# A selective-scan layer with experts: the sum over states moved from GpSimd adds to accumulating DMAs

## The chip, the cores and the metric

The kernel runs on one core of a Trainium2 chip. The metric is the device time of one execution in microseconds (us). The engines are named as in the profile: PE is TensorE (matrix products; PEld is its weight load), DVE is VectorE, ACT is ScalarE, POOL is GpSimd, SP is the engine that issues most DMAs.

## What is computed

The input x has 16 samples of 256 positions with 256 features, all float32. Each sample is normalised to xn, and the output is x plus a selective-scan branch plus a mixture of experts:

```python
proj = jnp.einsum('blh,he->bel', xn, W_in)
hidden, gate = jnp.split(proj, 2, axis=1)               # 512 features each
hidden = silu(causal_conv4(hidden, conv_kernel) + conv_bias)
ssm_p = jnp.einsum('ble,ed->bld', hidden.transpose(0, 2, 1), W_x)
dt, Bm, Cm = jnp.split(ssm_p, [128, 128 + 16], axis=-1)
dts = softplus(jnp.einsum('blr,re->ble', dt, W_dt) + b_dt)
dA  = exp(dts[..., None] * A)                           # A = -exp(A_log), 16 states
dBu = dts[..., None] * Bm[:, :, None, :] * hidden_ble[..., None]
# over positions: state = dA * state + dBu;  y = sum over the 16 states of state * Cm
y = (y + hidden * D) * silu(gate)
branch = jnp.einsum('bel,eh->blh', y, W_out)
# experts: 32 of them, 96 wide, the 8 most probable per position, weights renormalised;
# each adds ((silu(xn @ w_gate) * (xn @ w_up)) @ w_down) * weight
out = x + branch + experts
```

## The kernel before, in words

Samples are worked on one after the other, with the preparation of a sample laid under the scans of the one before. The 512 features of the scan are four chunks of 128 partitions, and the 256 positions lie along the free dimension. All experts are computed for all positions, as 24 chunks of 128 hidden features in 12 pairs (q), issued in 6 batches of two pairs.

The scan of a sample is cut into 16 units. A unit is one chunk c and one group g of NG = 4 states; a unit has two halves (h) of two states. One half is one slot of the plan, so a sample has 32 slots. For each unit:

- `fetch` has SP broadcast the rows of B (tile br) and of C (tile cr) of a group from a DRAM copy (bcd) to all partitions, 512 KB each.
- `feed` (L487) on POOL multiplies br by the chunk of hs, which `inputs` (L467) has turned from hidden to dts * hidden; the result is bu.
- `decay` (L502) on ACT writes exp(dts * A) of two states into a PSUM tile da. There are three of these (AHEAD = 3).
- `scan` (L511) on DVE runs the recurrence over a half in place in da, 512 elements a partition. The first position of each state has its decay forced to zero, which parts the two states.
- `read` (L522) on DVE multiplies da by cr into a half of the SBUF tile pr.
- `collect` (L536, L537, L538) on POOL adds the four states of pr to each other and to y: first 512 elements, then 256, then 256 into y. The tile y begins as hidden * D, written by `skip` (L462) on ACT.

After a sample's scans, `gate` (L546) makes the gate projection on PE into a PSUM bank, `gate_silu` (L555) applies SiLU in place on ACT, `gated` (L559) multiplies it into y on DVE, `project_out` (L565) adds the product with W_out on PE into the accumulator acc, and `finish` (L572) adds the x tile xt and stores the result. The accumulator also takes the experts' output (`down`, L374). The experts' products are made by `expand` (L343: pg and pu), `silu` (L351), `combine` (L356) and `weigh` (L362), which multiplies by the routing weights wr; `spread` (L329) broadcasts these from DRAM in six DMAs per quarter of the experts.

Before the scans of a sample: `stats`, `root`, `invert`, `norm`, `turn` (transposes, pt) and `keep_turned` (xnT) normalise it; `route`, `largest`, `expo`, `choose` route it; `project` (L385, ph), `conv_first` (L397, ACT) and `conv_rest` (L406, DVE) make the convolution into cv; `activate` (L413) writes hs; `params` (L422, px), `keep_params`, `widen` (L442, pdt) and `steps` (L454, dts by softplus) make the parameters.

The PSUM has three da tiles, two banks of kind g, two of kind u (`bank`), and acc. Products on PE share the g and u banks in turn, so a bank is free only when its reader is done: pgate of a sample is of kind u, like pu.

Each engine executes its own instructions in order. This order is written by hand: a dictionary WHEN gives each step a slot, relative to the first slot of its sample, and a rank inside the slot; the class Plan sorts by these and calls the steps. Nothing is reordered afterwards; the waits between engines follow from the tiles that the instructions read and write and from the number of buffers of the pools p1 to p4.

Of the kernel before, what the change touches and what calls it, by code (L numbers as in the profile page):

```python
# [34 lines left out]
def mamba_moe_kernel(  # L35
# [42 lines left out]
    NG = 4  # L78
    NH = 2
    HALVES = NG // NH  # L80
    AHEAD = 3
    GROUPS = N // NG
    UNITS = GROUPS * EC
    EPG = NE // GROUPS
    CPG = FC // GROUPS
    PAIRS = FC // 2
    BATCH = PAIRS // 6
    SLOTS = UNITS * HALVES
    SPG = EC * HALVES
    BATCH_AT = (8, 13, 19, 23, 29, 34)  # L90
# [4 lines left out]
        load_x=(-54, 34), stats=(-50, 35), root=(-49, 20), invert=(-48, 40), norm=(-47, 4),  # L95
        turn=(-46, 14), keep_turned=(-46, 14), route=(-39, 29), largest=(-38, 31), expo=(-37, 25),
        choose=(-37, 40), project=((-27, 32), (-24, 12)), conv_first=((-26, 4), (-24, 34)),
        conv_rest=((-24, 36), (-24, 20), (-22, 3), (-23, 35)), activate=(-22, 4), params=(-20, 10),
        keep_params=(-18, 9), turn_weights=(-19, 9), keep_weights=(-18, 11),
        widen=((-15, 9), (-13, 10)), steps=((-14, 34), (-13, 29)),  # L100
        skip=((-15, 8), (-9, 36), (-9, 16), (-9, 3)), inputs=(-7, 25), fetch=((-11, 8), (-6, 8)),
        spread=(6, 29), feed=(-2, 12), collect=(3, 34), gates=(1, 13), ups=(2, 9), silu=(2, 4),
        combine=((4, 8), (3, 34)), weigh=((5, 33), (4, 13)), down=(3, 14),
        gate=((27, 29), (33, 29)), gate_silu=((28, 14), (34, 6)), gated=((30, 31), (35, 34)),
        project_out=((37, 29), (39, 4)), finish=(47, 6),
# [20 lines left out]
    def load_x(b):  # L126
        xt = p4.tile([P, SPS, H], F32, tag="xt", name=f"xt_{b}")
        nc.sync.dma_start(xt, xf[ts(b, L), :].rearrange("(s p) h -> p s h", p=P))
        live["xt", b] = xt
# [34 lines left out]
    load_x(1)  # L164
# [226 lines left out]
    def conv_first(b, q):  # L391
        if q == 0:
            live["cv", b] = p1.tile([P, EC, L], F32, tag="cv", name=f"cv_{b}")
        cv, ph = live["cv", b], live["ph", b, q]
        for j in range(2):
            c = 2 * q + j
            nc.scalar.activation(  # L397
                cv[:, c, :], ph[:, j, :], AF.Identity,
                bias=cb[:, c, :], scale=cw[:, c, KC - 1 : KC],
            )  # L400

    def conv_rest(b, q, j):
        cv, ph = live["cv", b], live["ph", b, q]
        c = 2 * q + j
        for k in range(1, KC):
            nc.vector.scalar_tensor_tensor(  # L406
                cv[:, c, k:], ph[:, j, : L - k], cw[:, c, KC - 1 - k : KC - k],
                cv[:, c, k:], op0=ALU.mult, op1=ALU.add,
            )

    def activate(b):
        hs = p2.tile([P, EC, L], F32, tag="hs", name=f"hs_{b}")
        nc.scalar.activation(hs, live.pop(("cv", b)), AF.Silu)  # L413
        live["hs", b] = hs
# [43 lines left out]
    def skip(b, c):  # L458
        hs = live["hs", b]
        if c == 0:  # L460
            live["y", b] = p2.tile([P, EC, L], F32, tag="y", name=f"y_{b}")
        nc.scalar.activation(live["y", b][:, c, :], hs[:, c, :], AF.Copy, scale=dsk[:, c, :])  # L462
# [9 lines left out]
    def fetch(b, g, i):  # L472
        rep = p2.tile([P, NG, L], F32, tag="bc"[i] + "r", name=f"{'bc'[i]}r_{b}_{g}")
        rows = live["bcd", b][i * N + g * NG : i * N + (g + 1) * NG, :]
        nc.sync.dma_start(
            rep.rearrange("p n l -> p (n l)"),
            rows.rearrange("n l -> (n l)").partition_broadcast(P),
        )
        live["rep", b, g, i] = rep

    def unit(k):
        return k // UNITS, k // EC % GROUPS, k % EC

    def feed(k):
        b, g, c = unit(k)
        bu = p3.tile([P, NG, L], F32, tag="bu", name=f"bu_{b}_{g}_{c}")
        nc.gpsimd.tensor_mul(  # L487
            bu, live["rep", b, g, 0],
            live["hs", b][:, c : c + 1, :].to_broadcast([P, NG, L]),
        )  # L490
        live["bu", k] = bu

    def decay(m):
        k, h = divmod(m, HALVES)
        if k >= B * UNITS:
            return
        b, g, c = unit(k)
        dts = live["dts", b]
        da = ps_d.tile([P, NH, L], F32, tag="da", name=f"da_{b}_{g}_{c}_{h}")
        for j in range(NH):  # L500
            n = g * NG + h * NH + j
            nc.scalar.activation(  # L502
                da[:, j, :], dts[:, c, :], AF.Exp, scale=a_sb[:, c, n : n + 1]
            )
        live["da", m] = da

    def scan(m):
        k, h = divmod(m, HALVES)
        da = live["da", m]
        flat = da.rearrange("p n l -> p (n l)")  # L510
        nc.vector.tensor_tensor_scan(  # L511
            flat, flat, live["bu", k][:, ts(h, NH), :].rearrange("p n l -> p (n l)"), 0.0,
            op0=ALU.mult, op1=ALU.add,
        )

    def read(m):
        k, h = divmod(m, HALVES)
        b, g, c = unit(k)
        if h == 0:
            live["pr", k] = p3.tile([P, NG, L], F32, tag="pr", name=f"pr_{b}_{g}_{c}")  # L520
        cr = live["rep", b, g, 1]
        nc.vector.tensor_mul(  # L522
            live["pr", k][:, ts(h, NH), :], live.pop(("da", m)), cr[:, ts(h, NH), :]
        )
# [7 lines left out]

    def collect(k):
        b, g, c = unit(k)
        pr, y = live.pop(("pr", k)), live["y", b]
        nc.gpsimd.tensor_add(pr[:, 0:2, :], pr[:, 0:2, :], pr[:, 2:4, :])  # L536
        nc.gpsimd.tensor_add(pr[:, 0, :], pr[:, 0, :], pr[:, 1, :])  # L537
        nc.gpsimd.tensor_add(y[:, c, :], y[:, c, :], pr[:, 0, :])  # L538
# [14 lines left out]
    def gate_silu(b, q):  # L553
        pg = live["pgate", b, q]
        nc.scalar.activation(pg, pg, AF.Silu)  # L555

    def gated(b, q):
        y = live["y", b]
        nc.vector.tensor_mul(y[:, ts(q, 2), :], live.pop(("pgate", b, q)), y[:, ts(q, 2), :])  # L559

    def project_out(b, q):
        y, acc = live["y", b], live["acc", b]
        for c in range(2 * q, 2 * q + 2):
            for s in range(SPS):
                nc.tensor.matmul(  # L565
                    acc[:, s, :], y[:, c, ts(s, P)], wout_sb[:, c, :],
                    start=False, stop=False, skip_group_check=True,
                )

    def finish(b):  # L570
        o = p2.tile([P, SPS, H], F32, tag="o", name=f"o_{b}")
        nc.vector.tensor_add(o, live.pop(("acc", b)), live.pop(("xt", b)))  # L572
# [6 lines left out]
    def put(base, step, *args, i=None):  # L579
# [11 lines left out]
        project_out=project_out, finish=finish, feed=feed, collect=collect,  # L591
# [10 lines left out]
    for k in range(B * UNITS):  # L602
        put(HALVES * k, "feed", k)
        put(HALVES * k, "collect", k)
    for m in range(B * T + 1):
        plan.at(m, 30, advance, m)
    for b in range(B):
        s = T * b
        if b > 1:
            put(s, "load_x", b)  # L610
        for step in (
            "stats", "root", "invert", "norm", "turn", "keep_turned", "route", "largest", "expo",
            "choose", "activate", "params", "keep_params", "turn_weights", "keep_weights",
            "inputs", "finish",
        ):
            put(s, step, b)
        for q in range(2):
# [4 lines left out]
            for step in ("gate", "gate_silu", "gated", "project_out"):  # L622
# [3 lines left out]
        for g in range(GROUPS):  # L626
            for i in range(2):
                put(s + SPG * g, "fetch", b, g, i, i=i)
            put(s + SPG * g, "spread", b, g)
# [43 lines left out]
```

## Time and profile before

| | |
|---|---|
| median of 3 runs | 1440.61 us (1440.57 to 1440.69) |
| the profiled execution | 1441.18 us |
| its span, first to last instruction | 1439.4 us |
| mean granted PE clock | 0.987 |
| busy: PE / DVE / ACT / POOL | 1310.8 / 1284.4 / 1134.4 / 1319.7 us |
| feed, L487 | 256 of 2358 ns on POOL |
| collect, L536 / L537 / L538 | 256 each of 1271 / 727 / 726 ns on POOL |
| scan, L511, and read, L522 | 512 each of 1222 and 673 ns on DVE |
| table loads of ACT | 302 of 1283 ns |
| moved by DMA | 139.78 MB, 97 GB/s over the span |

The times of the table are of one profiled execution, and busy time is the union of an engine's instructions. An engine that is busy most of the time need not be the one that sets the pace; for that its waits, and the work just in front of them, have to be read in a stretch of the steady part.

### The profile page before, as it was taken

The numbers are of one execution on the slowest core, as the hardware profiler recorded it, in microseconds if no ns is written. First come the engines' busy times: TensorE is split into PE (matmuls) and PEld (weight loads), VectorE is DVE, ScalarE is ACT, GpSimd is POOL, SyncE is SP. The second block draws the span as 40 slices with busy tenths as digits, with TensorE's granted clock in tenths as the row PEclk, the third lists the DMA queues.
The fourth block names the chain that finished last, engine by engine and source line by source line (L and its number), as shares of the span: only waits on it lengthen the run. The fifth ranks groups of instructions, "written<-read, shape, count | busy, mean of one in ns | idle before, by whom it ended". The sixth has DMA issues, their size and how long they took to land.

```text
span 1439.4 us, 18685 instructions
## 1 busy us (share of the span) xinstructions
PE 1310.8 (91%) x5986; PEld 1108.0 (77%) x5986; DVE 1284.4 (89%) x1937; ACT 1134.4 (79%) x1904; POOL 1319.7 (92%) x1063
## 2 busy tenths in 40 slices
PE   4499999999999999999999999999999999998988
PEld 2378777887878778787887877878787877877867
DVE  2699999899998999999899999999999899998983
ACT  3688787978879788787978878888887978868762
POOL 0799999999999999999999999999999999999993
PEclk9699999999999999999999999999999999999999
DMA  6842432332332332332333232332232233233230
GB/s 193 227 127 67 119 88 74 112 88 88 97 96 75 109 98 79 107 100 77 97 99 101 74 113 80 88 112 85 86 103 81 91 110 97 66 112 88 68 101 8
DMA packets 108274, 139.78 MB, mean 97 GB/s; under 512 B 28656, under 2 KB 91152, under 8 KB 108176
## 3 DMA queue, kind: packets, MB, share of 16 engines
q1 hardware_dynamic: 105536, 138.55, 32.0%
q8 instruction: 47, 0.77, 0.2%
q10 hardware_dynamic: 2640, 0.05, 0.1%
q14 instruction: 51, 0.42, 0.1%
HBM read 133.31 MB, written 5.24 MB: 96 GB/s over the span
## 4 chain that ended last, share of the span: by engine, by line
PE 57%; DVE 14%; ACT 12%; POOL 12%; issue 3%; DMA 1%; SPq 0%; ACTq 0%; POOLq 0%
PE pu L343 17%; PE acc L374 17%; PE pg L343 12%; POOL bu L487 5%; DVE da L511 5%; PE px L422 4%; DVE pr L522 4%; ACT da L502 4%; POOL pr L536 3%; DVE cv L406 3%; PE acc L565 2%; PE pgate L546 2%; PE ph L385 2%; POOL pr L537 2%; POOL y L538 2%
## 5 line engine op out<-in xcount | busy, mean ns | idle before, releaser
L511 DVE TENSOR_TENSOR_SCAN da<-da,bu 128x512 f32<-128x512 f32 x512 | 625.4, 1222 | 63.2 <-ACT da L502 42.9
L502 ACT ACTIVATE da<-dts,a_sb 128x256 f32<-128x256 f32 x1024 | 477.8, 475 | 212.6 <-DVE pr L522 189.6
L487 POOL TENSOR_TENSOR bu<-br,hs 128x1024 f32<-128x1024 f32 x256 | 603.5, 2358 | 0.0
L343 PE MATMUL pu<-xnT,wu_sb 128*128 128x256 f32 x1536 | 357.1, 382 | 45.7 <-DVE y L559 29.7
L343 PE MATMUL pg<-xnT,wg_sb 128*128 128x256 f32 x1536 | 357.7, 383 | 40.3 <-DVE cv L406 27.6
L343 PEld LDWEIGHTS pu<-xnT,wu_sb 128*128 128x128 f32 x1536 | 290.3, 191 | 97.1 <-DVE y L559 36.1
L343 PEld LDWEIGHTS pg<-xnT,wg_sb 128*128 128x128 f32 x1536 | 289.7, 191 | 90.4 <-issue 33.2
L374 PE MATMUL acc<-wd_sb,h 128*128 128x256 f32 x1536 | 349.7, 381 | 1.5 <-DVE o L572 1.5
L522 DVE TENSOR_TENSOR pr<-da,cr 128x512 f32<-128x512 f32 x512 | 344.7, 673 | 0.0
L536 POOL TENSOR_TENSOR pr<-pr 128x512 f32<-128x512 f32 x256 | 325.3, 1271 | 10.9 <-DVE pr L522 10.2
L374 PEld LDWEIGHTS acc<-wd_sb,h 128*128 128x128 f32 x1536 | 292.0, 191 | 41.0 <-issue 1.8
L537 POOL TENSOR_TENSOR pr<-pr 128x256 f32<-128x256 f32 x256 | 186.1, 727 | 20.1
L538 POOL TENSOR_TENSOR y<-y,pr 128x256 f32<-128x256 f32 x256 | 185.8, 726 | 20.1
L502 ACT ACT_TABLE_LOAD x140 | 179.6, 1283 | 2.5
L356 DVE TENSOR_TENSOR pu<-pu,sg 128x512 f32<-128x512 f32 x192 | 124.8, 689 | 18.1 <-PE pu L343 18.1
L362 DVE TENSOR_TENSOR h<-pu,wr 128x512 f32<-128x512 f32 x192 | 130.7, 681 | 9.3 <-PE acc L374 9.1
L351 ACT ACT_TABLE_LOAD x95 | 121.9, 1283 | 1.7
L351 ACT ACTIVATE sg<-pg 128x512 f32<-128x512 f32 x192 | 104.3, 595 | 3.3 <-PE pg L343 2.3
L406 DVE SCALAR_TENSOR_TENSOR cv<-ph,small,cv 128x255 f32<-128x255 f32 (+2 forms) x192 | 90.5, 479 | 6.9 <-ACT cv L397 1.0
L467 POOL TENSOR_TENSOR hs<-dts,hs 128x1024 f32<-128x1024 f32 x16 | 37.7, 2359 | 43.8 <-ACT y L462 43.8
L422 PE MATMUL px<-hs,wx_sb 128*32 128x256 f32 (+1 forms) x256 | 63.7, 397 | 7.4 <-ACT hs L413 7.4
L385 PE MATMUL ph<-xnT,win_sb 128*128 128x256 f32 x256 | 64.7, 400 | 0.3 <-ACT dts L454 0.3
(60 smaller groups left out, 782.4 us busy)
## 6 DMA issues: line engine op xcount, KB each, us to landing
br<-bcd SPq DMA_DIRECT2D x64, 512.0 KB, 4.0
cr<-bcd SPq DMA_DIRECT2D x64, 512.0 KB, 3.9
wr<-wd SPq DMA_DIRECT2D x128, 192.0 KB, 3.8
wr<-wd SPq DMA_DIRECT2D x128, 128.0 KB, 4.2
wr<-wd SPq DMA_DIRECT2D x128, 64.0 KB, 3.9
xt<-L_attn_input_states_dram SPq DMA_DIRECT2D x16, 256.0 KB, 4.4
out_dram<-o SPq DMA_DIRECT2D x16, 256.0 KB, 3.6
wg_sb<-in_L_ffn_w_gate_dram SPq DMA_DIRECT2D x8, 384.0 KB, 6.0
```

The costliest lines, as they stand in the source:

```text
L343: nc.tensor.matmul(p[:, j, :], w[:, hc, ts(c, P)], xs[:, hc, :], start=(hc == 0), stop=(hc == HC - 1),)
L351: nc.scalar.activation(sg, live.pop(("g", b, q)), AF.Silu)
L362: nc.vector.tensor_mul(h, live.pop(("u", b, q)), wr[:, r : r + 2, :])
L374: nc.tensor.matmul(acc[:, s, :], h[:, j, ts(s, P)], wd_sb[:, c, :], start=(c == 0 and s == 0), stop=(c == FC - 1), skip_group_check=True,)
L406: nc.vector.scalar_tensor_tensor(cv[:, c, k:], ph[:, j, : L - k], cw[:, c, KC - 1 - k : KC - k], cv[:, c, k:], op0=ALU.mult, op1=ALU.add,)
L487: nc.gpsimd.tensor_mul(bu, live["rep", b, g, 0], live["hs", b][:, c : c + 1, :].to_broadcast([P, NG, L]),)
L502: nc.scalar.activation(da[:, j, :], dts[:, c, :], AF.Exp, scale=a_sb[:, c, n : n + 1])
L511: nc.vector.tensor_tensor_scan(flat, flat, live["bu", k][:, ts(h, NH), :].rearrange("p n l -> p (n l)"), 0.0, op0=ALU.mult, op1=ALU.add,)
L522: nc.vector.tensor_mul(live["pr", k][:, ts(h, NH), :], live.pop(("da", m)), cr[:, ts(h, NH), :])
L536: nc.gpsimd.tensor_add(pr[:, 0:2, :], pr[:, 0:2, :], pr[:, 2:4, :])
L537: nc.gpsimd.tensor_add(pr[:, 0, :], pr[:, 0, :], pr[:, 1, :])
L538: nc.gpsimd.tensor_add(y[:, c, :], y[:, c, :], pr[:, 0, :])
```

## The change

A unit is now two states (NG = 2) by two chunks (CPU = 2), so a slot is one chunk with two states, and a sample has 8 groups of two units, again 16 units and 32 slots. The tile y is now two tiles (u = 0 and 1), each with two chunks and two planes, one plane for each state of a group. `collect` is one DMA issued by POOL, which adds the tile pr (512 KB) elementwise onto y in SBUF. Plane 0 begins as hidden * D, plane 1 is cleared by POOL (`clear`). After the last group, `fold` adds plane 1 to plane 0 on POOL. The gate's SiLU is written by ACT to an SBUF tile gs, and the gate product is made on POOL instead of DVE.

Also: the convolution is made in the tile hs itself, and cv is gone; br and cr are 256 KB each, twice as many, with three buffers instead of two; pr has four buffers instead of three; xt has one buffer instead of four, and the x for the final sum is loaded a second time (`load_again`) into the tile o, which has one buffer instead of two; the second sample's x is loaded from the plan instead of ahead of it. The routing weights stay in four parts. Most entries of WHEN are changed.

```diff
-    NG = 4
-    NH = 2
-    HALVES = NG // NH
+    NG = 2
+    CPU = 2
...
-    BATCH_AT = (8, 13, 19, 23, 29, 34)
+    BATCH_AT = (8, 13, 19, 23, 28, 34)
...
+        skip=((-15, 6), (-10, 35), (-9, 13), (-8, 4)), clear=(-6, 36), inputs=(-4, 9),
+        fetch=((-9, 35), (-5, 14)), spread=(3, 13), feed=(-3, 29), collect=(4, 29), gates=(1, 11),
+        ups=(2, 6), silu=(2, 11), combine=((4, 10), (3, 34)), weigh=((5, 34), (4, 13)),
+        down=(3, 29), gate=((27, 35), (34, 11)), gate_silu=((28, 10), (34, 12)),
+        fold=((34, 34), (37, 35)), gated=((36, 32), (40, 13)), project_out=((39, 60), (40, 60)),
+        load_again=(44, 11), finish=(48, 4),
...
-        xt = p4.tile([P, SPS, H], F32, tag="xt", name=f"xt_{b}")
+        xt = p1.tile([P, SPS, H], F32, tag="xt", name=f"xt_{b}")
...
+    def clear(b):
+        for u in range(PAIRED):
+            nc.gpsimd.memset(live["y", b, u][:, :, 1, :], 0.0)
...
-        rep = p2.tile([P, NG, L], F32, tag="bc"[i] + "r", name=f"{'bc'[i]}r_{b}_{g}")
+        rep = p3.tile([P, NG, L], F32, tag="bc"[i] + "r", name=f"{'bc'[i]}r_{b}_{g}")
...
         nc.gpsimd.tensor_mul(
-            bu, live["rep", b, g, 0],
-            live["hs", b][:, c : c + 1, :].to_broadcast([P, NG, L]),
+            bu, live["rep", b, g, 0].unsqueeze(1).to_broadcast([P, CPU, NG, L]),
+            live["hs", b][:, ts(u, CPU), :].unsqueeze(2).to_broadcast([P, CPU, NG, L]),
         )
...
     def collect(k):
-        b, g, c = unit(k)
-        pr, y = live.pop(("pr", k)), live["y", b]
-        nc.gpsimd.tensor_add(pr[:, 0:2, :], pr[:, 0:2, :], pr[:, 2:4, :])
-        nc.gpsimd.tensor_add(pr[:, 0, :], pr[:, 0, :], pr[:, 1, :])
-        nc.gpsimd.tensor_add(y[:, c, :], y[:, c, :], pr[:, 0, :])
+        b, g, u = unit(k)
+        nc.gpsimd.dma_start(
+            live["y", b, u].rearrange("p c n l -> p (c n l)"),
+            live.pop(("pr", k)).rearrange("p c n l -> p (c n l)"),
+            accum_op=ALU.add,
+        )
+
+    def fold(b, u):
+        y = live["y", b, u]
+        nc.gpsimd.tensor_add(y[:, :, 0, :], y[:, :, 0, :], y[:, :, 1, :])
...
     def gate_silu(b, q):
-        pg = live["pgate", b, q]
-        nc.scalar.activation(pg, pg, AF.Silu)
+        gs = p2.tile([P, 2, L], F32, tag="gs", name=f"gs_{b}_{q}")
+        nc.scalar.activation(gs, live.pop(("pgate", b, q)), AF.Silu)
+        live["gs", b, q] = gs
 
     def gated(b, q):
-        y = live["y", b]
-        nc.vector.tensor_mul(y[:, ts(q, 2), :], live.pop(("pgate", b, q)), y[:, ts(q, 2), :])
+        y = live["y", b, q][:, :, 0, :]
+        nc.gpsimd.tensor_mul(y, y, live.pop(("gs", b, q)))
...
+    def load_again(b):
+        o = p1.tile([P, SPS, H], F32, tag="o", name=f"o_{b}")
+        nc.sync.dma_start(o, xf[ts(b, L), :].rearrange("(s p) h -> p s h", p=P))
+        live["o", b] = o
```

## Prediction

> **What bounds the kernel now.** I read the profile in four steps: busy shares, the waits of a steady stretch, one cycle of the busiest engine, and the DMA queue.
>
> ```profile
> PE 1310.8 (91%) x5986; PEld 1108.0 (77%) x5986; DVE 1284.4 (89%) x1937; ACT 1134.4 (79%) x1904; POOL 1319.7 (92%) x1063
> ```
>
> Three engines are near 90%, so shares alone don't name the bound. The work repeats once per sample. In the chain of waits the px product of line 422 comes back at 421.55 and 850.33 us, five samples apart: one sample takes 428.78/5 = 85.76 us. For exactly those five samples, the table by stretch, then the waits of POOL, PE and DVE (us in total, times, longest):
>
> ```profile
> 421.55:850.30 428.75, 404.44 (x1871) 343.30 (x1872) 400.71 (x606) 354.86 (x595) 412.16 (x331) 1.00 0.31 93
> ...
> POOL pr L536 <- DVE pr L522: 3.5, 5, 0.7
> ...
> PE pu L343 <- DVE y L559: 8.8, 5, 1.8
> PE pdt L442 <- ACT xnT L256: 5.1, 5, 1.0
> PE pu L343 <- ACT sg L351: 4.4, 5, 0.9
> PE pg L343 <- DVE cv L406: 3.6, 5, 0.7
> PE pg L343 <- ACT dts L454: 2.5, 5, 0.5
> ...
> DVE da L511 <- ACT da L502: 13.9, 15, 2.2
> DVE pu L356 <- PE pu L343: 3.5, 5, 0.7
> DVE da L511 <- POOL bu L487: 3.4, 5, 0.7
> ```
>
> The columns of the first line are the stretch, its length, then busy us of PE, PEld, DVE, ACT and POOL, granted clock, DMA share and GB/s. Divided by five: PE 80.9, DVE 80.1, ACT 71.0, POOL 82.4 us of 85.76. POOL waits 0.7 us per sample, PE 4.9 and DVE some 5. The clock is full. POOL's remaining idle is no wait; the timeline of one unit on POOL (start, us) shows it:
>
> ```profile
> 597.38 2.36 POOL L487 TENSOR_TENSOR bu<-br,hs 128x1024 f32<-128x1024 f32 x1
> 599.70 1.27 POOL L536 TENSOR_TENSOR pr<-pr 128x512 f32<-128x512 f32 x1
> 601.05 0.73 POOL L537 TENSOR_TENSOR pr<-pr 128x256 f32<-128x256 f32 x1
> 601.85 0.72 POOL L538 TENSOR_TENSOR y<-y,pr 128x256 f32<-128x256 f32 x1
> 602.53 2.36 POOL L487 TENSOR_TENSOR bu<-br,hs 128x1024 f32<-128x1024 f32 x1
> ```
>
> The cycle is 5.15 us: 2.32 for the feed, 2.83 for the three dependent adds of collect. 16 units make 82.4, the product of line 467 with its memset 2.5, the wait 0.7: 85.6, the whole sample. POOL sets the period. PE and DVE are close behind. The last view, the DMA queue and the landing time of the largest transfers (KB each, us from issue to landing):
>
> ```profile
> q1 hardware_dynamic: 105536, 138.55, 32.0%
> ...
> br<-bcd SPq DMA_DIRECT2D x64, 512.0 KB, 4.0
> ```
>
> The 16 DMA engines are two thirds idle.
>
> **The change part by part**, per sample unless said.
>
> Removed from POOL: the 16 collects, 16 x 2.83 = 45.3 us. Removed from DVE: two gate products, 2 x 0.68 = 1.36 us.
>
> Added to POOL: two folds and two gate products, four two-input operations of 512 elements a partition, nearest row L536 at 1.27: 5.1 us. Two clears of 512 elements: the memset of line 197 takes 0.20 us for 128 elements, so 0.2 to 0.8 each; I take 0.5, 1.0 in all. Then 16 accumulating DMAs, d us each of POOL's time. With feeds (37.1; same elements, two broadcast operands instead of one, taken as equal) and line 467 (2.5), POOL needs 45.7 + 16 d. No row has a DMA issued from POOL. From below: SP issues one in 0.34 us. From above: nothing in the trace; d = 2.83 would give back all that the adds freed per unit. [...]
>
> How long an accumulate takes to land matters because collect of one y waits, in POOL's in-order queue, for the accumulate two units earlier on the same y, and behind it stand the next feed and so the scan. Row first: a 512 KB broadcast lands in 4.0 us. By the queue line, 16 engines x 32.0% x 1439.4 us / 138.55 MB is 53 engine-us per MB, so 512 KB keep all 16 engines busy for 1.74 us of that. [...] A same-y pair of units is 4 slots of 2.6 us = 10.4 us, so it is hidden. [...] The pr tiles now come free at landing; with four buffers the next writer is five slots away, 13 us.
>
> The gate product on GpSimd: the row is 0.68 us on DVE (L559) against 1.27 on POOL (L536). [...] It also ends PE's longest steady wait: pgate's bank is freed by the SiLU on ACT instead of by the later product, so "pu <- DVE y", 8.8/5 = 1.8 us, goes. What is late next in that place is the SiLU itself, two table loads of 1.28 us round it as before; the number of table loads is 302 in both programs.
>
> Moves: the retuned table moves most steps by a few ranks. Instruction counts on PE are the same (5986) and on ACT too. SP issues 64 + 64 more, smaller broadcasts and 16 second loads of x: 144 x 0.34 = 49 us over the run on a queue that mostly waits for buffers (now three deep), so nothing; if a broadcast came late the feed would wait, and a prefetch of six slots (15 us) covers a landing of 4 to 9. x on one buffer is loaded after the previous norm; its row is due 6 slots later. cv now in hs: nothing.
>
> Next bound. PE: 80.9 busy plus its waits without the one removed, 3.1: 84.0. DVE: 80.1 - 1.4 + waits 2.8 (ACT, round the softplus table loads) + about 1.6 (PE): 83.1; its wait for bu, 0.7, goes. Some of each engine's waits are for the other and shrink when POOL lets ACT and DVE run earlier. The floor is 80.9 and the sum 84; I take 82.9, so 2.9 us off each of about 15.5 periods (the last one already runs partly without feeds): 45 us. Start: the second sample's convolution moves one scan step earlier, 1.7 us, and the second x load sits behind five weight loads but is needed 10 us after it lands: -2. End: the last accumulate lands 3 to 4 us later than the adds ended, but PE still has 13.8 us of expert products ahead of project_out there, so fold and gate (2.5 us) fit: +1 to 3. These cancel. The profiled execution took 1441.18 us (span 1439.4 and 1.8 around it), 0.6 above the median 1440.61. From it 1441.2 - 45 = 1396, and 0.6 less against the median; 1396.
>
> **The rivals.**
>
> DMA-bound (slower). The accumulates do not land within the 10.4 us of a pair. [...] Against: DMA share is only 0.31 now and the broadcast lands in 4.0. It decides from landing plus issue = 10.7 us, or from 3.5 us of all engines per accumulate; each us beyond costs 8 us a sample. At 11.5 us: 8 x 11.5 = 92 a sample, 6 more over 15.5, 1535; a mild case with engines at 3.7 us gives 87 a sample, 1460.
>
> POOL stays the bound. d is 2.3 to 2.8 instead of 1: 45.7 + 16 x 2.5 = 85.7, no change; 2.4 gives 84.1 and 1415. For: nothing in the trace prices it. Against: 2.5 is seven times SP's issue.
>
> PE and DVE hold each other. The waits stay at today's size in another order: 84.3 a sample, 1418. Or they vanish: 81.6, 1376. These are the ends of the main case.
>
> The sums not leaving POOL at all (the accumulate split into more POOL instructions) is unlikely: the queue shows one DMA in the place of three adds.
>
> **How the numbers follow.** Forecast (POOL freed, period 81.6 to 84.3): 0.69, 1376 to 1418, at 1396. POOL still the bound: 0.10, 1405 to 1450 (0.04 of it faster, 0.04 within 0.2%, 0.02 slower). DMA-bound: 0.19, 1450 to 1600. Others, slower: 0.02. Measurement tells about 0.2% (3 us) from no change. Faster: 0.69 + 0.04 = 0.73; same 0.04; slower 0.19 + 0.02 + 0.02 = 0.23. The range leaves out the lowest few of the first case and the worse part of the DMA case: 1372 to 1470; the likeliest case alone is 1376 to 1418.
>
> **What would show it.** POOL busy near 750 us and no longer waiting for nothing; gaps of about 1 us where DMAs are issued; px every 82.9 us; "pu <- DVE y" gone; PE's busy share 94% or more; accumulates landing in 5 to 8 us; DMA share near 0.7 to 0.8. Wrong: POOL waiting on y's accumulates for more than a few us a sample, scans waiting on bu, DMA share above 0.9, or POOL gaps above 2.3 us at each DMA.

## The result, and the profile after

The changed kernel takes 1435.83 us (median, 1432.76 to 1438.63), against 1440.63 us for the kernel before beside it on the same chip. The ratio is 0.9968, with a 95% interval of 0.9957 to 0.9979: 0.3% faster, where 3.1% was forecast. The sign was right, but by luck, as the end of this section shows: the steady samples, where the 45 us were to come from, gave nothing.

Four lines of the profile's page of the changed kernel: the busy shares, the queue of POOL's DMAs (packets, MB, share of 16 engines), the accumulating DMA on POOL, and its landing time.

```profile
PE 1317.3 (92%) x5986; PEld 1108.5 (77%) x5986; DVE 1265.7 (88%) x1905; ACT 1135.2 (79%) x1904; POOL 958.9 (67%) x647
...
q0 software_dynamic: 36864, 134.23, 49.0%
...
L538 POOL DMA_DIRECT2D y<-pr x256 | 241.0, 942 | 201.2 <-DVE pr L526 179.0
...
y<-pr POOLq DMA_DIRECT2D x256, 512.0 KB, 6.5
```

Everything that the change was to do to POOL happened: its share fell from 92% to 67%, an accumulate costs POOL 0.94 us and lands in 6.5 us. Yet PE and DVE are no busier than before. The pace shows in a steady stretch. One sample runs from one copy of bc on ACT (L430) to the next, and the stretch below, by the table of stretches and the waits of PE and DVE (us in total, times, longest), is three samples long.

```profile
426.19:683.13 256.94, 243.84 (x1124) 205.57 (x1123) 237.05 (x358) 212.99 (x358) 179.77 (x121) 1.00 0.85 195
...
PE pu L344 <- DVE hs L407: 7.8, 3, 2.6
PE pg L344 <- ACT dts L454: 1.4, 3, 0.5
PE ph L386 <- DVE h L363: 1.4, 3, 0.5
PE pdt L442 <- ACT xnT L257: 1.1, 3, 0.4
...
DVE da L516 <- ACT da L508: 9.8, 12, 2.2
DVE da L516 <- POOL y L568: 3.9, 3, 1.3
DVE h L363 <- PE acc L375: 2.9, 3, 1.0
DVE pu L357 <- PE pu L344: 1.5, 3, 0.5
```

A sample takes 256.94/3 = 85.65 us. Before it took 85.75. POOL is busy for 59.9 us of it instead of 82.4, and the sample is 0.1 us shorter. This is the regular sample; some of the changed kernel's samples are longer, up to 86.87 us (last section), and the mean from its second to its last copy is 85.96 us, against 85.80 before. PE's wait for the gate product, 1.8 us a sample, is gone, and in its place PE waits 2.6 us for the last convolution (L407). DVE still waits 3.3 us for ACT's exponentials; the 1.3 us that are put down to POOL's gate product are ACT's too, for in the kernel without table loads below that row is gone although POOL makes the same product.

So where do the 5 us come from? ACT's line 430 in both kernels (before and then after; each line gives the start of the first and of the last copy):

```profile
L430 ACT COPY bc<-px x16: 357/357/361, 35.2 to 1283.2; 32x256 f32<-32x256 f32 x16
```

```profile
L430 ACT COPY bc<-px x16: 357/357/363, 35.1 to 1285.6; 32x256 f32<-32x256 f32 x16
```

Up to the last copy the changed kernel is 2.4 us late; after it, it needs 148.3 us to its end (span 1433.9) where the kernel before needed 156.2 (span 1439.4). The whole gain lies behind the last copy, where the last sample's scans run without a next sample beside them. There POOL held the pace before, as the waits of DVE in the kernel before show, from 1283.18 to the end:

```profile
DVE da L511 <- POOL bu L487: 9.0, 8, 1.6
```

Against 0.7 us a sample in the steady part, 9.0 us in the last one. The first experiment below confirms it: with less work on POOL and nothing else changed, this stretch shrinks from 156.2 to 147.1 us. The prediction had put the end down as a loss of 1 to 3 us.

### The profile page after: what moved, and what is told of

It reads as the page before. It is cut to its first block, busy times and chain, and to the rows that moved or that the text cites. A ratio compares the mean times of both kernels' runs of the same rounds, so it can differ in the third digit from the quotient of the medians.

```text
span 1433.9 us, 19162 instructions
## 1 busy us (share of the span) xinstructions
PE 1317.3 (92%) x5986; PEld 1108.5 (77%) x5986; DVE 1265.7 (88%) x1905; ACT 1135.2 (79%) x1904; POOL 958.9 (67%) x647
## 3 DMA queue, kind: packets, MB, share of 16 engines
q0 software_dynamic: 36864, 134.23, 49.0%
## 5 line engine op out<-in xcount | busy, mean ns | idle before, releaser
L492 POOL TENSOR_TENSOR bu<-br,hs 128x1024 f32<-128x1024 f32 x256 | 638.2, 2493 | 213.3 <-DVE da L516 146.1
L538 POOL DMA_DIRECT2D y<-pr x256 | 241.0, 942 | 201.2 <-DVE pr L526 179.0
L407 DVE SCALAR_TENSOR_TENSOR hs<-ph,small,hs 128x255 f32<-128x255 f32 (+2 forms) x192 | 91.8, 479 | 5.6 <-ACT hs L398 1.0
L472 POOL TENSOR_TENSOR hs<-dts,hs 128x1024 f32<-128x1024 f32 x16 | 41.7, 2608 | 42.5 <-ACT y L463 42.5
L568 POOL TENSOR_TENSOR y<-y,gs 128x512 f32<-128x512 f32 x32 | 62.8, 1963 | 0.2
L422 PEld LDWEIGHTS px<-hs,wx_sb 128*32 128x32 f32 (+1 forms) x256 | 36.4, 152 | 34.0 <-issue 9.5
```

What stands on the lines that cost most here:

```text
L407: nc.vector.scalar_tensor_tensor(cv[:, c, k:], ph[:, j, : L - k], cw[:, c, KC - 1 - k : KC - k], cv[:, c, k:], op0=ALU.mult, op1=ALU.add,)
L422: nc.tensor.matmul(p, w[:, c, :], hs[:, c, :], start=(c == 0), stop=(c == EC - 1))
L492: nc.gpsimd.tensor_mul(bu, live["rep", b, g, 0].unsqueeze(1).to_broadcast([P, CPU, NG, L]), live["hs", b][:, ts(u, CPU), :].unsqueeze(2).t ...
L538: nc.gpsimd.dma_start(live["y", b, u].rearrange("p c n l -> p (c n l)"), live.pop(("pr", k)).rearrange("p c n l -> p (c n l)"), accum_op=A ...
```

## The experiments

**First set: does POOL hold the period, and do the accumulates cost anything?** Totals are to be read beside 1440.87 us, the kernel before on that chip.

*The kernel before with a lighter POOL.*

```diff
     def collect(k):
-        nc.gpsimd.tensor_add(pr[:, 0:2, :], pr[:, 0:2, :], pr[:, 2:4, :])
-        nc.gpsimd.tensor_add(pr[:, 0, :], pr[:, 0, :], pr[:, 1, :])
         nc.gpsimd.tensor_add(y[:, c, :], y[:, c, :], pr[:, 0, :])
```

> The kernel before with the two first adds of collect left out (one of four states is summed, so the output is not the reference's): 33 us of POOL work less per sample, nothing else moved. Theory A (the order of PE, ACT and DVE, with its waits on one another, is itself a ring about as long as POOL's 85.7 us, so that freeing POOL frees little): 1425 to 1438 us, sample period 85.0 to 85.7. Rival B (POOL alone was the bound of the kernel before, and what it freed was spent by the changed kernel's own costs: the accumulates' DMA load or its new order): period near 83 to 84, 1395 to 1415 us.

Measured: 1430.70 us, ratio 0.9925 (0.9909 to 0.9942). The stretch of three samples, one wait of PE and two of DVE in it:

```profile
424.33:681.58 257.25, 242.67 (x1124) 205.82 (x1123) 240.45 (x364) 212.88 (x358) 153.07 (x103) 1.00 0.31 93
...
PE pu L343 <- DVE y L557: 5.3, 3, 1.8
...
DVE da L511 <- ACT da L502: 8.4, 9, 2.2
DVE da L511 <- POOL y L536: 2.0, 3, 0.7
```

POOL is busy for 51 us a sample instead of 82.4, and the sample still takes 257.25/3 = 85.75 us, with the same waits of PE and DVE to the tenth. Even the 0.7 us a sample that DVE had seemed to wait for POOL's bu are there, now put down to another instruction of POOL, so POOL was not their cause. Some 9 of the 10 us are the tail again: 147.1 us behind the last copy. POOL's 85 us of gapless work had only just fitted under a period that others set.

*The changed kernel without its accumulating DMAs.*

```diff
     def collect(k):
-        nc.gpsimd.dma_start(
-            live["y", b, u].rearrange("p c n l -> p (c n l)"),
-            live.pop(("pr", k)).rearrange("p c n l -> p (c n l)"),
-            accum_op=ALU.add,
-        )
+        live.pop(("pr", k))
```

> The changed kernel without the accumulating DMAs (y is left at hidden * D): DMA share back from 0.85 to about 0.37, POOL down by 256 x 0.94 us, no wait on their landing. Theory A (ring of PE, ACT and DVE): within 0.3% of the changed kernel, 1431 to 1437 us. Rival B (the accumulates and the DMA traffic set the pace, through late br and cr or POOL's queue): 1400 to 1420 us.

Measured: 1435.26 us, ratio 0.9958 (0.9943 to 0.9973), the changed kernel within its scatter. The 241 us of issue on POOL, the 49% of the DMA engines and the landing of 6.5 us are all hidden. Three regular samples of this kernel:

```profile
427.10:684.03 256.93, 243.85 (x1124) 205.57 (x1123) 237.05 (x358) 212.96 (x358) 138.00 (x73) 1.00 0.31 97
```

PE, DVE and ACT are as in the changed kernel's stretch above; only POOL, with 46.0 us a sample instead of 59.9, and the DMA share, 0.31 instead of 0.85, are not.

*The changed kernel with the last convolution earlier*, at the wait that took the old one's place.

```diff
-        conv_rest=((-24, 12), (-25, 11), (-22, 3), (-24, 60)),
+        conv_rest=((-24, 12), (-25, 11), (-24, 61), (-24, 60)),
```

> The changed kernel with one entry of its order table moved: the last chunk's conv_rest directly behind the one before, two slots earlier on DVE. It takes the end of that step from behind two scan steps, which is what PE waits 2.6 us per sample for (pu behind the bank of ph). Theory A (PE's waits are part of the ring that sets the period): 1 to 2 us per sample less, 1405 to 1422 us. Rival B (DMA or POOL sets the pace): PE waits elsewhere, no change within 0.3%. Rival C (DVE sets the pace through ACT's table loads): no change, the wait of PE only moves.

Measured: 1462.57 us, ratio 1.0147 (1.0132 to 1.0163), slower; the samples take 86.8 us, or 88.25 where PE's clock fell for a moment (9 of 14; the mean clock of the profiled run is 0.973; last section). In one of 86.81 us, at full clock, the wait is down from 2.6 to 0.9 us, but PE now waits 2.2 us for dt and 0.9 us for h. The wait was not a loss to be removed by itself: removed at one place, it came back at others, with more.

*The changed kernel with the old order of the steps*: WHEN and BATCH_AT as before for the steps of PE, ACT and DVE from `stats` to `gate_silu`, but for `skip`; the rest as changed. Some of the entries, lines shortened:

```diff
-    BATCH_AT = (8, 13, 19, 23, 28, 34)
+    BATCH_AT = (8, 13, 19, 23, 29, 34)
...
-        conv_rest=((-24, 12), (-25, 11), (-22, 3), (-24, 60)), activate=(-22, 8),
+        conv_rest=((-24, 36), (-24, 20), (-22, 3), (-23, 35)), activate=(-22, 4),
...
-        gate=((27, 35), (34, 11)), gate_silu=((28, 10), (34, 12)),
+        gate=((27, 29), (33, 29)), gate_silu=((28, 14), (34, 6)),
```

> The changed kernel with the order table of before for the steps of PE, ACT and DVE (normalise, route, convolve, parameters, experts, gate and its SiLU), and its own for the steps of POOL, SP and the output. Theory A: PE's wait for y is gone and no new one is put in its place, so the period is 82.5 to 84.5 us and the time 1390 to 1418. Rival C (DVE and ACT set the pace in either order): within 0.5% of the changed kernel, 1428 to 1442. Rival D (the new order is what lets the changed kernel gain anything): slower than before, above 1443.

Measured: 1427.79 us, ratio 0.9906 (0.9891 to 0.9920), so the new order of the steps, on its own, costs some 8 us here. The regular period is 85.57, nearly the same. Of the 8 us, 5 lie before the last copy: the profiled execution of the changed kernel has samples of 86.87 and 86.1 us among those of 85.65, some 5 us in all (more on these at the end), and the old order has none; the rest is the tail, 145.5 against 148.3 us. The old order's chain is as closed as the new one: PE's 1.8 us for the gate product went, and PE waits elsewhere (the line numbers of this kernel are 29 higher behind WHEN):

```profile
424.77:681.48 256.71, 242.53 (x1124) 206.07 (x1123) 236.90 (x358) 213.20 (x358) 179.97 (x121) 1.00 0.86 195
...
PE pgate L583 <- DVE h L392: 4.1, 3, 1.4
```

**Second set: which of the other engines holds it?** Each of three kernels takes work from one engine of the changed kernel and leaves order and handoffs alone. The kernel before took 1442.58 us on that chip.

*One table on ACT.*

Every Silu and the Sqrt become Identity, the Softplus becomes Exp; two of the five places:

```diff
-        nc.scalar.activation(sg, live.pop(("g", b, q)), AF.Silu)
+        nc.scalar.activation(sg, live.pop(("g", b, q)), AF.Identity)
...
-                dts[:, c, :], pv[:, j, :], AF.Softplus, bias=bdt[:, c, :]
+                dts[:, c, :], pv[:, j, :], AF.Exp, bias=bdt[:, c, :]
```

> The changed kernel with Silu and Sqrt replaced by Identity and Softplus by Exp, so that ScalarE stays in one table: about 300 loads of 1283 ns, 24 us of ScalarE per sample of 85.65 us, are gone; the instructions of the other engines and their order are the same. The values that flow are not the reference's. Theory A (TensorE, VectorE and ScalarE hold each other in a ring, and ScalarE's table loads lie in it at four or five handoffs of a sample): the sample's period falls to 80 to 83 us, bounded below by TensorE's 81.5 us of matmuls; the total is 1360 to 1395 us. Rival B (the period lies between TensorE and VectorE alone, and ScalarE's loads are hidden): period 85.3 to 85.7, total within 5 us of the changed kernel's 1436. Rival C (VectorE is held by its own work, 79 us and its start-up gaps): period 84 to 85.3.

Measured: 1412.47 us, ratio 0.9790 (0.9776 to 0.9805), period 85.18. The stretch, PE's waits and DVE's longest:

```profile
415.56:671.12 255.56, 245.28 (x1124) 210.03 (x1123) 236.46 (x358) 139.30 (x300) 179.64 (x121) 0.98 0.86 196
...
PE pu L344 <- DVE hs L407: 7.2, 3, 2.4
PE pdt L442 <- ACT xnT L257: 3.0, 3, 1.0
...
DVE h L363 <- PE acc L375: 7.1, 9, 1.1
```

ACT's busy time falls by 24.6 us a sample, the period by 0.47. Now PE has no idle time but these two waits: 245.28/3 + 2.4 + 1.0 = 85.2. DVE's wait for ACT's exponentials is gone; its longest is now for PE.

But 0.47 us is not what the table loads are worth. The clock of PE, 1.00 in the changed kernel's stretch, is 0.98 here: in nearly every sample it falls for a moment, at a loss of 1.7 us (last section). The two steady samples without a fall take 83.50 and 83.75 us. One of them, and one with a fall:

```profile
161.94:245.44 83.50, 80.07 (x376) 68.83 (x375) 78.69 (x120) 46.30 (x101) 59.85 (x41) 1.00 0.88 199
500.75:585.93 85.18, 81.75 (x376) 70.00 (x375) 78.78 (x120) 46.43 (x100) 59.87 (x41) 0.98 0.85 196
```

PE's busy time differs by what the fall costs, and the sample by the same. So at full clock the table loads are worth some 2 us of period, most of which the clock took back.

The rest of the 23 us lies in the start, where the first two copies come 3 and 6 us earlier, in the tail (142.1 us instead of 148.3), and in the missing long samples. Theory A's 80 to 83 failed, and rival C had the number without the cause, since DVE now idles 6 us a sample.

*A lighter PE*: in every other pair the second chunk's down product is left out. That is 24 records a sample; 16 of them are issued in 3.45 us in the timeline, so it takes 5.2 us (the expectation had 4.6).

```diff
-        for j in range(2):
+        for j in range(1 if q % 2 == 0 else 2):
             c = 2 * q + j
```

> The changed kernel without the second half of the down product of every other pair: 24 matmuls of 383 ns fewer in each sample, wait for wait the same; the output lacks those terms. That is 12 matmuls a sample for each of its two row blocks, so 24 x 0.383 = 9.2 us of TensorE at most if the two row blocks count apart, 4.6 us if the pair count is six with two matmuls each. Theory A (ring): the period falls by a part of it only, to 83 to 84.5 us, total 1395 to 1420. Rival B (TensorE alone is the bound, its 81.5 us and the waits that come of its own bunching): the period falls by all that was taken, to 81 us or less, total below 1365. Rival C (VectorE or ScalarE sets the period): nothing, 85.3 to 85.7.

Measured: 1421.95 us, ratio 0.9864 (0.9847 to 0.9880), period 85.29. The stretch, and all the longer waits of DVE:

```profile
421.50:677.36 255.86, 235.09 (x1052) 194.47 (x1051) 236.77 (x358) 213.50 (x357) 179.54 (x121) 0.98 0.86 195
...
DVE da L517 <- ACT da L509: 9.8, 12, 2.2
DVE pu L357 <- PE pu L344: 3.9, 3, 1.3
DVE da L517 <- POOL y L569: 3.9, 3, 1.3
```

PE gets 5.2 us less to do and the period loses 0.36. Now it is DVE that has no idle time but its waits: 236.77/3 = 78.9, plus 4.6 for ACT and 1.3 for PE, 84.8 of 85.3, the rest in waits too short for these rows. PE's clock falls here too, to a mean of 0.98 over the stretch; what the period would be without it is not known.

*A lighter DVE*: the product of up and activated gate over half of its columns, 12 a sample of 423 instead of 691 ns, 3.2 us.

```diff
-        pu = live["u", b, q]
-        nc.vector.tensor_mul(pu, pu, live.pop(("sg", b, q)))
+        pu = live["u", b, q][:, :, : L // 2]
+        nc.vector.tensor_mul(pu, pu, live.pop(("sg", b, q))[:, :, : L // 2])
```

> The changed kernel with the product of up and activated gate made over half of its columns: 12 products a sample shorter by about 0.3 us each, 3.5 us of VectorE a sample, every handoff kept; the other half of the columns is left without its gate. Theory A (ring): period 83.5 to 85 us, total 1410 to 1428. Rival B (VectorE alone is the bound): period down by all 3.5, to 82.1, total 1380 or less. Rival C (TensorE or ScalarE sets the period): 85.3 to 85.7, total within 5 us of 1436.

Measured: 1435.55 us, ratio 0.9956 (0.9941 to 0.9970), period 85.64: nothing, as rival C had it.

*Fewer table loads without leaving anything out*: the gate's SiLU beside a batch's, on the old order.

```diff
-        gate=((27, 29), (33, 29)), gate_silu=((28, 14), (34, 6)),
+        gate=((24, 12), (35, 12)), gate_silu=((25, 3), (36, 3)),
```

> The changed kernel with the old order of the steps (as in the earlier run, 1428 us, period 85.57) and, on top, the gate's activation moved beside the batch's activations (gate at slots 24 and 35, its Silu at 25 and 36, just ahead of the batch's own), so that both share one load of the table: four table loads fewer in a sample, 5.1 us of ScalarE. Nothing is left out. Theory A: VectorE's waits for ScalarE's exponentials shrink and the period falls to 84 to 85.3 us, total 1405 to 1425. Rival B (ScalarE's loads are hidden): 85.4 to 85.7, total within 3 us of 1428. Rival C (the gate's product ahead of the batch delays the batch, and the ring with it): period 86 or more, total above 1433.

Measured: 1474.04 us, ratio 1.0214 (1.0176 to 1.0253), periods of 87.7 us, and of 89.4 where PE's clock fell (a mean of 0.99 over the three samples from 438.13 us). Two waits of PE over these three samples say why:

```profile
PE pgate L583 <- DVE h L392: 6.6, 3, 2.2
PE pu L373 <- ACT gs L592: 6.0, 3, 2.0
```

The gate's product at its new place waits for a bank of kind u that DVE frees late, and the batch's second up product then waits for the gate's SiLU in the bank after it. The expectation's rival C held; the table loads saved (62 in the run) are not seen.

**Third set: two chains side by side?** About half a per cent of the period from each of two cuts, nothing from the third, suggested two chains of nearly equal length: PE with its waits, and DVE with ACT's table loads. Two cuts at once tell that from a third holder. The kernel before took 1443.01 us on that chip.

*One table and a lighter PE together, on the changed kernel* (the two edits above), *and the same on the kernel before*.

> The changed kernel with both of the earlier cuts at once: no table switches (24.4 us of ScalarE a sample) and 12 matmuls a sample fewer in the down product (4.6 us of TensorE). The values are not the reference's. Alone, the first gave a period of 85.18 us, where TensorE had no idle time but 3.4 us a sample in two waits; the second gave 85.29, where VectorE had no idle time but 4.6 us for ScalarE and 1.3 for TensorE. Theory A' (two chains side by side, TensorE with its two waits, and VectorE with ScalarE's table loads, each close to 85.2 us, so that either alone moves the period by under 0.5): both cuts together give 80.5 to 83 us, total 1345 to 1385. Rival B (a third thing that none of the cuts touched, a queue or GpSimd, holds the period at 85.2): 84.9 to 85.3, total 1400 to 1420.

> The kernel before with the same two cuts as in the run on the changed kernel (no table switches, 12 matmuls a sample fewer in the down product); values are not the reference's. GpSimd's 85.05 us of work a sample are untouched here. Theory A': GpSimd alone now holds the period, at 85.0 to 85.4 us, its waits gone; total 1420 to 1436. Then the difference to the changed kernel with the same cuts is what the change is worth once the two chains give way. Rival (GpSimd never binds): the same period as the changed kernel with these cuts, below 83.5.

Measured: the changed kernel 1346.98 us, ratio 0.9328 (0.9312 to 0.9344); the kernel before 1433.10 us, ratio 0.9934 (0.9919 to 0.9949). The stretches, the changed kernel's first:

```profile
401.66:641.14 239.48, 226.98 (x1052) 191.83 (x1051) 235.24 (x358) 139.19 (x301) 179.74 (x121) 1.00 0.92 209
```

```profile
419.54:677.53 257.99, 233.40 (x1052) 196.43 (x1051) 240.43 (x364) 139.02 (x302) 247.53 (x199) 0.97 0.30 93
...
DVE da L512 <- POOL bu L488: 9.1, 12, 1.0
...
POOL pr L537 <- DVE pr L523: 2.7, 3, 1.9
```

On the changed kernel the cuts gave 0.47 us (some 2 at full clock) and 0.36 us apart and 5.8 us together: 239.48/3 = 79.83, at full clock; with the samples in which the clock fell, the mean is 80.5. DVE is at 78.4 us of the 79.83, close to the next bound. On the kernel before the same cuts give nothing in the steady part: POOL works all but 0.9 us a sample, DVE waits for bu 3.0 us a sample where it had waited 0.7, and the period stays at 85.4 to 85.7, but for two samples of 87.1 (the stretch above ends with one; its mean clock is 0.97). Here, with the two chains out of the way, is what the change is worth: 86 us, 6%.

*The other two pairs of cuts, on the changed kernel.*

> The changed kernel with the 4.6 us of TensorE's down product and the 2.5 us of VectorE's half product left out together (the output lacks both); the table loads stay. Theory A': the chain of VectorE and ScalarE becomes shorter by VectorE's 2.5 us at most: period 82.7 to 84.3, total 1385 to 1412. Rival B (third holder at 85.2): 84.9 to 85.3, total 1412 to 1425.

> The changed kernel without table switches and with the half product of VectorE (2.5 us a sample less); values are not the reference's. Theory A': TensorE's chain is untouched but for its wait of 2.4 us for VectorE's convolution: period 84 to 85.2 us, total 1395 to 1412. If TensorE's wait is set by VectorE's order behind it and not by VectorE's load, the period stays at 85.1 to 85.2. Rival (VectorE's load holds the 85.18): 82.7, total below 1375.

Measured: PE and DVE lighter, 1410.84 us, ratio 0.9775 (0.9761 to 0.9790), periods 84.3 to 84.7; one table and DVE lighter, 1411.44 us, ratio 0.9787 (0.9772 to 0.9801), period 85.18 as with one table alone, and 83.50 in the one steady sample in which the clock did not fall (its mean over the three samples from 418.66 us is 0.98). The second says that the chain through PE doesn't depend on how much DVE has to do. The first says that the other chain isn't DVE's load either, for of the 3.2 us taken from DVE only 0.6 to 1 came out. This wait of DVE, over three samples, took most of the rest (9.8 before the cut):

```profile
DVE da L517 <- ACT da L509: 15.6, 14, 2.2
```

| taken from the changed kernel | period, us | total, us |
|---|---|---|
| nothing | 85.65 | 1435.8 |
| ACT's table loads | 85.18 (83.5 at full clock) | 1412.5 |
| 5.2 us of PE | 85.29 | 1422.0 |
| 3.2 us of DVE | 85.64 | 1435.6 |
| table loads and DVE | 85.18 (83.5 at full clock) | 1411.4 |
| PE and DVE | 84.3 to 84.7 | 1410.8 |
| table loads and PE | 79.83 (mean 80.5) | 1347.0 |

The runs were made on several chips; the kernel before took 1440.6 to 1443.0 us on them.

**Fourth set: are the chains a matter of the order?** The complete changed kernel with a new order of PE's, ACT's and DVE's steps, and the old order once more beside it. The kernel before took 1442.09 us. Some of the entries, lines shortened:

```diff
-    BATCH_AT = (8, 13, 19, 23, 28, 34)
+    BATCH_AT = (8, 13, 19, 24, 29, 34)
...
-        conv_rest=((-24, 12), (-25, 11), (-22, 3), (-24, 60)), activate=(-22, 8),
+        conv_rest=((-25, 33), (-24, 27), (-23, 42), (-23, 44)), activate=(-22, 16),
-        widen=((-14, 10), (-13, 6)), steps=((-14, 40), (-13, 9)),
+        widen=((-14, 38), (-13, 14)), steps=((-13, 23), (-13, 26)),
-        ups=(2, 6), silu=(2, 11), combine=((4, 10), (3, 34)), weigh=((5, 34), (4, 13)), down=(3, 29),
+        ups=(2, 37), silu=(2, 18), combine=((4, 12), (3, 37)), weigh=((7, 19), (4, 17)), down=(3, 35),
-        gate=((27, 35), (34, 11)), gate_silu=((28, 10), (34, 12)),
+        gate=((28, 44), (34, 12)), gate_silu=((29, 15), (34, 23)),
...
```

> The changed kernel, complete, with the table WHEN written anew for the steps of TensorE, VectorE and ScalarE: the two conversions of the step sizes stand next to each other at slot 19 behind both of their products, the batches' products are issued half a slot later (gates, ups and down at ranks 11, 37, 35), the second batch's weighing at slot 7 after its batch, the fourth batch one slot later, the gate's product behind the third batch's. GpSimd's steps and the DMAs are as in the changed kernel, but for x loaded three slots earlier. Theory A' (two chains, each some 4 to 6 us of waits above its engine's work, both formed by the order of the steps): an order that shortens the waits of both at once brings the period from 85.57 to 83.5 to 85 us and the total to 1395 to 1420. Rival (the waits belong to the table loads and to the buffers, and no order of the steps takes them away): a period of 85.3 or more, total 1424 or more.

> The changed kernel with the old order of the steps once more, on the same chip as the new order, as its measure: 1428 within 3 us by the earlier run.

Measured: the new order 1422.22 us, ratio 0.9861 (0.9844 to 0.9877); the old one 1431.13 us, ratio 0.9921 (0.9905 to 0.9938), 3.3 us above the first run and so just outside of what was expected. The new order's stretch, and the longest waits of PE and of DVE:

```profile
427.58:681.52 253.94, 243.88 (x1124) 205.60 (x1123) 236.59 (x358) 212.78 (x358) 179.63 (x121) 1.00 0.87 197
...
PE pu L344 <- DVE hs L407: 4.5, 3, 1.5
...
DVE da L516 <- ACT da L508: 8.4, 9, 2.2
```

The period is 84.65, a full us less with every operation in place: PE's wait for the convolution fell from 2.6 to 1.5 us, and no sample behind the third copy is longer than 84.66. The start is 6 us longer (the third copy comes at 173.6 us, in the changed kernel at 167.6). At 1.4% below the kernel before, this is the fastest complete version of the study. So part of the waits is the order's. What stays, DVE's 2.2 us behind the softplus and its two table loads, stood in each of the orders.

## Why the prediction was right and wrong

- **"POOL sets the period" failed**, the first step. Its arithmetic was right: 85.05 us of work and 0.7 of waits fill the sample. But an engine without idle time is only as long as the period; it need not make it. The lighter POOL shows that the period is 85.75 us with 31 us less on POOL. The forecast took 2.9 us off each period for it; measured were 0.1 off the regular sample, and 0.2 more in the mean. The evidence was in the lines shown: POOL did wait, 0.7 us a sample for pr, and DVE's wait for POOL's bu was no longer than that, while PE and DVE had 5 us of waits for each other and for ACT.
- **The next bound, 82.9 us, failed.** The sum took the waits of PE and DVE as slack that shrinks once POOL is gone. In the changed kernel they are parts of two chains: PE with 81.3 us busy and 4.3 of waits, 85.6, and DVE with 79.0 busy, 4.6 of waits for ACT and 1.5 for PE, 85.1. The two are not independent, for without table loads PE's chain shrinks as well, to 83.5 at full clock. Which step of one hands its lateness to which step of the other was not followed through. The rival "PE and DVE hold each other" had the mechanism (waits of today's size "in another order"); it took off the 1.8 us for the gate product, which came back as 2.6 us for the convolution. ACT was missing from it as a member of a chain, for at 71 us of 85.76 it looked idle.
- **The price of the accumulates came out near the forecast, but no run stood behind it.** The kernel before issues no DMA from POOL and none that adds. The gaps of about 1 us, the landing in 5 to 8 us and the DMA share of 0.7 to 0.8 were the author's estimate, and so was the 1 us against which a rival sets its 2.3 to 2.8. Measured: POOL 0.94 us each; landing 6.5; DMA share 0.85; POOL's work 59.9 us a sample, the DMAs counted (the 750 us named for the run had left these out: 958.9 - 241.0 = 718). The queue line gives 16 x 49.0% x 1433.9 / 134.23 = 84 engine-us per MB, 2.7 us of all 16 engines for 512 KB. Against the 53 of the broadcasts before it is 1.6 times as much.
- **The DMA-bound rival** fell with the kernel without accumulates: same time. No run showed the 11.5 us of landing and issue, or the 3.7 us of all engines, at which it was costed; measured were 6.5 + 0.94 and 2.7.
- **The gate product and the small operations on POOL were sized right, though their rows say otherwise.** The rows of the changed kernel have 1.96 us for a gate product and 1.70 for a fold against the 1.27 assumed, 0.81 for a clear against 0.5 and 2.49 for a feed against 2.32. In the kernel without accumulates the same instructions take 1.27, 1.27, 0.53 and 2.36 us, and POOL is busy for 46.0 us a sample where the prediction had 45.7. Beside the accumulates POOL's records overlap: the fold (L546) starts before the DMA issue in front of it has ended, and the feed (L492) starts 1.24 us behind the fold.

```profile
561.96 0.88 POOL L538 DMA_DIRECT2D y<-pr  x1 [2.63 <-DVE pr L526]
562.57 1.57 POOL L546 TENSOR_TENSOR y<-y 128x512 f32<-128x512 f32 x1
563.81 2.64 POOL L492 TENSOR_TENSOR bu<-br,hs 128x1024 f32<-128x1024 f32 x1
```

- **"Start and end cancel" was wrong**: the start was even, and the end gave 7.9 us instead of costing 1 to 3. That the last accumulate lands 3 to 4 us after the adds had ended was shown by no run; in the changed kernel's run the median landing is 6.5 us, against 2.83 us for the three adds before, and the end became shorter all the same. This alone made the kernel faster, so the right sign was luck. POOL's bound in the last sample, DVE's 9.0 us for bu, stood in the trace of before; averaged over five steady samples it did not show.
- **The new order was costed at nothing.** Against the old one, on the same changed kernel, it costs 7 to 9 us by the two runs, each set against the kernel before on its own chip (ratios of 0.9906 and 0.9921 against 0.9968), most of it through the long samples.

## What to carry to other kernels

An engine that is busy without a gap is not thereby the bound: take work from it, or find out who waits for it, before forecasting from the next engine's busy time. Where several engines hand work to each other in a fixed order, a cut on one of them shows little while another chain is as long; cutting two at once is the test, and here 0.47 and 0.36 us became 5.8. Compare the clock of the stretches before pricing a cut: most of what one cut was worth had gone into a lower clock (samples of 85.18 us at 0.98 against 83.50 at 1.00). Read the tail by itself, for what binds there may not bind in the steady part.

## What the runs showed of the hardware

PE's granted clock fell after some short pauses and not after others. In the one-table kernel PE pauses 2.4 us in each sample (the first line below holds most of it, no matmul), and just behind it the clock is at 0.58:

```profile
572.80:575.00 2.20, 0.00 (x0) 0.01 (x1) 2.13 (x6) 1.04 (x3) 2.03 (x1) 1.00 1.08 249
575.20:578.40 3.20, 3.20 (x10) 2.56 (x10) 3.20 (x5) 2.64 (x6) 1.50 (x3) 0.58 1.00 258
```

By the timeline, the eight matmuls behind the pause take 3.09 us and the sixteen after them 4.22, against 1.97 and 3.62 at full clock: 1.7 us. But the two steady samples of 83.50 and 83.75 us have the same pause and lose nothing. Two pauses of 2.42 us of the same kernel, each as the stretch that holds most of it and the stretch behind:

```profile
998.96:1002.37 3.41, 1.40 (x7) 1.27 (x8) 3.34 (x6) 2.47 (x5) 2.29 (x1) 1.00 1.03 220
1002.37:1005.79 3.42, 3.42 (x10) 2.70 (x9) 3.09 (x5) 2.32 (x6) 2.87 (x2) 0.50 0.98 265
...
1084.29:1087.70 3.41, 1.54 (x7) 1.42 (x8) 3.34 (x7) 2.61 (x5) 2.15 (x1) 1.00 1.07 230
1087.70:1091.11 3.41, 3.41 (x17) 3.00 (x17) 3.41 (x6) 2.17 (x5) 2.98 (x2) 1.00 0.97 255
```

Behind the first the clock is at 0.50, behind the second it stays at 1.00.

In the changed kernel it is the same. From 70.95 us to the last copy its trace has three falls, each to half the clock for 3.41 us, and a clock of 1.00 between them:

```profile
70.95:330.30 259.35, 242.88 (x1117) 204.27 (x1116) 239.17 (x361) 215.50 (x361) 181.46 (x121) 1.00 0.88 204
330.34:333.74 3.40, 3.40 (x10) 2.69 (x9) 3.31 (x5) 3.37 (x5) 2.61 (x2) 0.50 0.85 201
...
333.75:760.40 426.65, 404.39 (x1864) 341.29 (x1863) 391.93 (x591) 351.93 (x591) 296.94 (x199) 1.00 0.85 193
760.41:763.82 3.41, 3.41 (x9) 2.67 (x9) 3.17 (x5) 3.35 (x6) 2.75 (x2) 0.50 1.05 245
763.83:1275.81 511.98, 485.32 (x2236) 409.48 (x2236) 470.84 (x710) 422.47 (x710) 356.55 (x239) 1.00 0.84 193
1275.83:1279.23 3.40, 3.40 (x9) 2.70 (x9) 3.37 (x5) 3.37 (x5) 2.54 (x2) 0.50 0.97 224
```

Each begins 1.1 to 1.3 us behind the end of PE's pause of 2.59 us for the last convolution. Here are the eight matmuls behind this pause in a sample without a fall, and in one with a fall:

```profile
587.79 1.97 PE L344 MATMUL pu<-xnT,wu_sb 128*128 128x256 f32 x8 [2.59 <-DVE hs L407]
...
759.09 2.48 PE L344 MATMUL pu<-xnT,wu_sb 128*128 128x256 f32 x8 [2.59 <-DVE hs L407]
```

The samples with a fall are 86.87 us long where a regular one is 85.65, and the sample behind one is 86.1. The scatter of the changed kernel's runs, 6 us, goes with the clock: 0.988 in the fastest and 0.982 in the slowest. In the three samples of the new order's stretch, with a pause of 1.5 us in each, the clock is at 1.00, and so it is in the kernel before, with a pause of 1.8 us, from 75 to 1279.7 us. Why one pause is followed by a fall and another of the same length is not was not shown.
